# A two-layer transformer kernel on one Trainium2 core: layer 1's attention in pairs of units, and a new order of loads and steps in its end part

## The chip, the cores and the metric

The kernel runs on one core of a Trainium2 chip. A core has five engines with a queue each: TensorE (PE; its weight loads are listed as PEld), VectorE (DVE), ScalarE (ACT), GpSimd (POOL) and SyncE (SP). Each engine executes its own list of instructions in order, and waits on semaphores for the others. Matmuls write to PSUM, which has eight banks of 2 KB for each of 128 partitions. The metric is the time of one launch on the device in microseconds (us); lower is better.

## What is computed

The reference is two transformer layers on x of shape (8, 256, 128), all in float32. A small matmul gives six vectors per batch element and layer, a shift s, a scale c and a gate g for each half:

```python
h = _layernorm(x, axis=-1) * (1 + ca) + sa
x = x + ga * _L0_attn_ref(h, ...)            # 16 heads of width 8, causal
h = _layernorm(x, axis=-1) * (1 + cb) + sb
x = x + gb * _L0_ffn_ref(h, ...)             # shared expert and the best 2 of 8
...
x = x + ga * _L1_attn_ref(h, w_q, w_k, w_v, w_o)   # 16 heads of width 64, causal
...
x = x + gb * _L1_ffn_ref(h, ...)             # h, shared expert, and the best 2 of 16
```

Layer 1's attention, which the change is about, is

```python
q = einsum('bsd,hqd->bhsq', x, w_q); k = ...; v = ...
scores = einsum('bhsq,bhtq->bhst', q, k)
weights = softmax(where(causal, -inf, scores) / sqrt(64), axis=-1)
cat = einsum('bhst,bhtv->bhsv', weights, v).transpose(0, 2, 1, 3).reshape(b, s, -1)
return einsum('bsf,df->bsd', cat, w_o)
```

Layer 1's expert network has 16 experts of width 64, gates from a sigmoid, and the two best chosen per token.

## The kernel before, in words

x lies in SBUF in four tiles of 512 tokens (two batch elements each), and h, the normalised input, lies turned, with features on the partitions. The two layers run one after the other; from layer 0's attention on, the order on every engine is the order in which the program writes its steps (`tc.manual_schedule()`).

**Layer 1's attention.** A unit is a quarter of the heads (four) of one batch element; B = 8 elements of 4 units give N = 32 units, numbered n = 4b + u. For each unit there are these steps:

- `project_qk1(b, u)`: q and k for four heads, 128x128 weights against 256 columns of h; each result takes one PSUM bank of the two with tag "p". VectorE copies q to SBUF and ScalarE copies k.
- `project_v1(b, u)`: a quarter of v, one matmul of 512 columns into a "p" bank; ScalarE copies it.
- `scores1(b, u, between)`: for each m of two pairs of heads, two matmuls side by side in the array (64 rows each) for each of two blocks of keys, into a tile "sc" of two banks (tag "s", two buffers: four banks). ScalarE takes the Exp into "pt", and POOL sets what lies above the diagonal to zero (`causal`, line 804). `between` holds steps which are put between the four causal instructions in POOL's list: gathers and scatters, set up with `at_head`.
- `values1(b, u)`: o = v times pt, 64 columns of the array each (tag "o", one bank), and the sums of pt with a matrix of ones, 32 columns each (tag "sum", one bank, which adds up over the four units of b). VectorE copies o to "ou".
- `reciprocals1(b)` takes r = 1 / sum (VectorE), writes r to DRAM ("rd") and reads it back spread over the partitions ("rb", one buffer); `judge(r)` keeps a flag on its range. `normalise1(b, u)` multiplies ou by rb, and `finish1(b)` multiplies by the output weights (y, line 1639, 32 matmuls) and adds to x.

The loop over n writes: scores1(n), project_qk1(n+2), the `early` steps, values1(n-1), project_v1(n+2), reciprocals1 where a batch element is done, the `ends` steps. `early` and `ends` hold layer 0's last combines, the layernorms (`measure` and `normalise` on VectorE and ScalarE, `modulate` with transposes "nt" on TensorE and the way back to SBUF on VectorE), the normalisations and projections of finished elements, and the router: `route1` is a generator whose steps (`go`) are the logits "lg", the choice of two experts on VectorE, their ranks "rk", and scatters of the tokens into xs, sorted by expert (POOL, line 916).

**The end part.** Tokens of the first six elements go through 40 tiles of 128 sorted rows, four tiles to a step m = 0 to 9 (NQ = 10). The first 16 tiles belong to the 16 experts with weights in SBUF. The others belong to whichever expert has more rows; `tables_steps` works out their experts (widx) and rows (rowi). `fetch_rows1(m)` loads rows (SyncE), `find_rows1(m)` loads the rows' places into SyncE's registers one by one, and `fetch_weights1(m)` loads experts' weights of 128 KB: for m = 4, 5 by SyncE with a register loaded ahead of each DMA, for m = 6 to 9 by POOL with indirect DMAs (line 1030). Then `turn1(m)` (transposes, and the fetch of rows m+4), `hidden1(m)`, `project_tiles(m)` (writes ys by SyncE). When all of ys is written, POOL gathers each token's two rows (`gather1`, 24 indirect DMAs, line 1038) and `combine1` adds them. The last two elements go through all experts densely: `norms`, `go6`/`go7` (their routers), `gate_rows`, `dense_hidden`, `dense_gate`, `dense_project`, `ffn1_add`. After the loop all these steps stand in one list written out by hand.

Of the kernel before, what the change touches and what calls it, by code (L numbers as in the profile page):

```python
# [16 lines left out]
P = 128  # L17
# [540 lines left out]
def fast_path(ctx: ExitStack, tc: tile.TileContext, i: dict, out: bass.AP, bad: bass.AP):  # L558
# [292 lines left out]
    class Sorted:  # L851
# [163 lines left out]
        def row_start(self, d):  # L1015

            return nc.values_load(
                self.rowi[0:1, d : d + 1], engines=[mybir.EngineType.SP], min_val=0,
                max_val=self.ne * self.cap - P,
                skip_runtime_bounds_check_because="clamped above, and not negative",  # L1020
            )

        def load_rows(self, xg, d, r=None):

            r = self.row_start(d) if r is None else r
            nc.sync.dma_start(out=xg, in_=self.xs[bass.ds(r, P), :])
# [500 lines left out]
    def project_qk1(b, u):  # L1527

        hb = batch_cols(h, b)
        for what, copy in (("q", nc.vector.tensor_copy), ("k", nc.scalar.copy)):  # L1530
            ps_ = ps_ln([P, 2, S], f"{what}p1_{b}_{u}")
            for n in range(2):
                nc.tensor.matmul(  # L1533
                    out=ps_[:, n, :], lhsT=w1[f"w{what}1"][:, bass.ts(2 * u + n, P)], rhs=hb, start=True, stop=True
                )
            st1[what, b, u] = lp.tile([P, 2, S], F32, tag=what, bufs=3, name=f"{what}1_{b}_{u}")
            copy(st1[what, b, u], ps_)  # L1537
# [16 lines left out]
    def scores1(b, u, between):  # L1554

        q, k = st1.pop(("q", b, u)), st1.pop(("k", b, u))
        for m in range(2):
            c = 2 * u + m
            sc = pp.tile([P, 2, 512], F32, tag="s", name=f"sc1_{b}_{c}")
            pt = lp.tile([P, 2, 384], F32, tag="pt", bufs=4, name=f"pt1_{b}_{c}")  # L1560
# [14 lines left out]
    def values1(b, u):  # L1575
        v = st1["v", b, u // 2]
        if u == 0:
            st1["s", b] = pp.tile([P, S], F32, tag="sum", bufs=1, name=f"sum1_{b}")
            st1["ou", b] = lp.tile([P, 2, 4, S], F32, tag="ou", name=f"ou1_{b}")
        s = st1["s", b]  # L1580
        o = pp.tile([P, 2, S], F32, tag="o", bufs=1, name=f"o1_{b}_{u}")
        pts = [st1.pop(("pt", b, 2 * u + m)) for m in range(2)]
        for m in range(2):
            for kb, cols, qs in blocks:
                for n in range(2):
# [3 lines left out]
                    )  # L1589

        for kb, cols, qs in blocks:
# [6 lines left out]
        nc.vector.tensor_copy(st1["ou", b][:, :, u, :], o)  # L1598

    def reciprocals1(b):  # L1600
# [14 lines left out]
        judge(r)  # L1615
# [112 lines left out]
    def find_rows1(m):  # L1728

        starts.extend(z1.row_start(4 * m + t - E1) for t in range(4))  # L1730

    def fetch_weights1(m):
# [3 lines left out]
        for t in range(4):  # L1736
            d = 4 * m + t - E1
            if m > 5:
                z1.load_weights(wt[:, t, :], i["wpk1"], d)
                continue  # L1740
            r = nc.values_load(
                z1.widx[0:1, d : d + 1], engines=[mybir.EngineType.SP], min_val=0, max_val=(E1 - 1) * P,
                skip_runtime_bounds_check_because="an expert's number, 128 times",
            )
            nc.sync.dma_start(out=wt[:, t, :], in_=i["wpk1"][bass.ds(r, P), :])
# [135 lines left out]
    def gather1(j):  # L1881
        k, n = divmod(j, 3)
        if n == 0:
            sums["yg", k] = lp.tile([P, 3, 2, P], F32, tag="pt", bufs=4, name=f"yg1_{k}")
# [39 lines left out]
    project_v1(0, 0)  # L1924
    project_qk1(0, 1)
    project_v1(0, 1)
    measure, normalise, modulate = layernorm_parts(0, md[1], SA, CA, "1a1", ps_ln, tiles=range(2, TT))
    at_end(0, lambda: combine(1), measure)
    at(1, normalise)
    at_end(1, modulate)  # L1930
# [3 lines left out]
    at_end(1, lambda: combine(2))  # L1934
    at_end(2, lambda: combine(3))
    for w in range(1, NW):
        n = 8 * w
        if w > 1:
            for k in range(4):
                at_head(n - 13 + k, 3, lambda w=w, k=k: gather(2 * w + k // 2, k % 2))  # L1940
            at_end(n - 9, lambda w=w: combine(2 * w))
            at_end(n - 8, lambda w=w: combine(2 * w + 1))
        measure, normalise, modulate = first_norm(w)
        n -= 7 if w > 1 else 6
        at_end(n, measure)
        at(n + 1, normalise)
        at_end(n + 1, modulate)
    for b in range(B - 1):
        n = 4 * b + 6 if b < B - 2 else N - 1
        at(n, *[lambda b=b, u=u: normalise1(b, u) for u in range(4)])  # L1950
        at_end(n, lambda b=b: finish1(b))
    for bs in ((0, 2), (2, 2), (4, 1), (5, 1)):
        n = 4 * sum(bs) + 2
        measure, normalise, modulate, tokens, add = norm1(bs)
        go = one(route1(bs))
        at_end(n, measure)
        at(n + 1, normalise)
        at_end(n + 1, modulate, tokens)
        at(n + 2, go)
        at_end(n + 2, go, go, go, go)  # L1960
        at_end(n + 3, go)
# [222 lines left out]
```

## Time and profile before

| | |
|---|---|
| median of 14 runs | 639.73 us (637.33 to 644.71) |
| the profiled execution | 641.42 us |
| its span, first to last instruction | 639.4 us |
| mean granted TensorE clock | 0.948 |
| packets and bytes moved by DMA | 51377, 85.45 MB, mean 134 GB/s |

Stages of the span: layer 0 until about 280 us, layer 1's attention from the first scores at 289.98 to 538.9, the 40 tiles until the last ys lands at about 585.6, and the gathers and the dense part from there to the end. From 340 to 500 us TensorE is busy for 158.1 of 160 us (in the stretch 404 to 436 for 30.53 of 32), at the full clock.

In the page a line of instructions is: start in us, length in us, engine, line of the program, operation, output tile <- input tiles, rows*columns of the array, shape, count, and in square brackets the engine's idle time before it with what ended it. Neighbouring instructions of one kind are merged. SPq and POOLq are the queues' own DMA issues. A float32 matmul shows as two MATMUL instructions.

### The profile page before, as it was taken

How to read it: one execution, taken by the hardware profiler on the slowest of the kernel's cores; microseconds unless marked ns; L12 is line 12 of the kernel's file. 1: busy time of each engine (PE TensorE's matmuls, PEld its weight loads, DVE VectorE, ACT ScalarE, POOL GpSimd, SP SyncE). 2: the span in 40 equal slices, each digit the busy share in tenths (PEclk: the TensorE clock that was granted, in tenths of full speed). 3: DMA queues.
4: the chain of work that ended last, by engine and by line, in shares of the span. 5: the costliest groups of instructions: out<-in, count | busy, mean ns of one | idle time of the engine just before them, and what ended most of it. 6: DMA issues, size and time to landing. Idle time of an engine off the chain costs nothing.

```text
span 639.4 us, 12934 instructions
## 1 busy us (share of the span) xinstructions
PE 565.2 (88%) x4903; PEld 402.6 (63%) x4903; DVE 350.1 (55%) x1055; ACT 288.7 (45%) x502; POOL 307.0 (48%) x454
## 2 busy tenths in 40 slices
PE   3798988988869999969999999999999996797973
PEld 3444544455569999756667676767776765675443
DVE  4335658677663222145743666566647575546486
ACT  2477665555505555426633453344434441442230
POOL 7234457576631444136561144752355647612773
PEclk9999898888989999989999999999999999889797
DMA  8999970012033999522030203030303035742441
GB/s 285 350 408 395 389 262 22 14 55 92 26 116 92 330 328 332 169 99 83 26 88 6 68 10 84 30 80 1 68 23 80 18 72 168 206 118 78 105 100 71
DMA packets 51377, 85.45 MB, mean 134 GB/s; under 512 B 6428, under 2 KB 30108, under 8 KB 50156
## 3 DMA queue, kind: packets, MB, share of 16 engines
q1 hardware_dynamic: 42140, 57.67, 28.2%
q0 software_dynamic: 9168, 26.88, 13.3%
q8 instruction: 40, 0.66, 0.4%
q14 instruction: 29, 0.24, 0.1%
HBM read 53.46 MB, written 31.07 MB: 132 GB/s over the span
## 4 chain that ended last, share of the span: by engine, by line
PE 39%; DVE 7%; POOL 3%; issue 3%; DMA 2%; ACT 2%; SPq 1%; DVEq 0%; POOLq 0%; ACTq 0%
PE sc L1564 7%; PE o L1586 6%; PE qp L1533 5%; PE vp L1546 5%; PE kp L1533 4%; PE y L1639 4%; POOL yg L1038 3%; PE sum L1594 3%; DMA yg<-ys,yidx 1%; PE gu L1771 1%; DMA xg<-xs 1%; PE xT L1760 1%; DVE tc L1894 1%; DVE a L1838 1%; PE rp L1627 1%
## 5 line engine op out<-in xcount | busy, mean ns | idle before, releaser
L804 POOL TENSOR_SCALAR_AFFINE_SELECT pt<-pt 128x256 f32<-128x256 f32 (+1 forms) x176 | 89.0, 531 | 135.4 <-ACT pt L1567 80.0
L1038 POOL DMA_INDIRECT yg<-ys,yidx x56 | 53.4, 954 | 54.3 <-issue 34.1
L1030 POOL DMA_INDIRECT wt<-in_wpk_dram,widx x47 | 44.3, 942 | 54.8 <-PE xT L1312 48.5
L1567 ACT ACTIVATE pt<-sc 128x768 f32<-128x768 f32 x64 | 48.4, 808 | 25.5 <-PE sc L1564 25.4
L1134 ACT ACTIVATE pt<-sc 128x1024 f32<-128x1024 f32 x48 | 46.5, 1020 | 28.0 <-PE sc L1130 27.9
L1323 ACT ACTIVATE hst<-hp,wt 128x128 f32<-128x128 f32 x136 | 38.8, 368 | 29.8 <-ACT hst L1323 20.9
L1564 PEld LDWEIGHTS sc<-q,k 64*128 64x128 f32 x512 | 41.6, 187 | 16.4 <-issue 11.4
L1564 PE MATMUL sc<-q,k 64*128 64x256 f32 (+1 forms) x512 | 50.5, 337 | 0.0
L1586 PE MATMUL o<-pt,v 128*64 128x256 f32 (+1 forms) x512 | 48.7, 332 | 1.7 <-POOL pt L804 1.7
L1549 ACT COPY v<-vp 128x512 f32<-128x512 f32 x32 | 18.7, 585 | 67.5 <-PE vp L1546 56.7
L1586 PEld LDWEIGHTS o<-pt,v 128*64 128x64 f32 x512 | 31.9, 137 | 19.6 <-POOL pt L804 5.5
L1333 DVE COPY ysb<-yt 128x128 f32<-128x128 f32 x39 | 11.4, 292 | 59.0 <-PE yt L1329 59.0
L1537 DVE COPY q<-qp 128x512 f32<-128x512 f32 x32 | 22.0, 688 | 38.5 <-PE qp L1533 38.5
L1321 PE MATMUL hp<-xTs,wt 128*128 128x128 f32 x272 | 36.7, 278 | 2.3 <-DMA wt<-in_wpk_dram,widx 1.4
L1533 PE MATMUL qp<-h,wq 128*128 128x256 f32 x128 | 37.1, 414 | 1.3 <-DVE sh L1282 1.3
L916 POOL DMA_INDIRECT xs<-ht0b,idx x32 | 31.5, 983 | 13.0 <-issue 4.6
L1546 PE MATMUL vp<-wv,h 128*128 128x512 f32 x64 | 35.9, 643 | 1.1 <-DVE q L1537 1.1
L1130 PE MATMUL sc<-qm,k 32*128 32x512 f32 x192 | 34.4, 745 | 2.6 <-ACT pt L1134 1.8
L1329 PE MATMUL yt<-wt,hst 128*128 128x128 f32 x272 | 35.8, 276 | 0.0
L1321 PEld LDWEIGHTS hp<-xTs,wt 128*128 128x128 f32 x272 | 33.0, 192 | 3.9 <-DVE xTs L1314 1.5
L1533 PE MATMUL kp<-h,wk 128*128 128x256 f32 x128 | 33.5, 385 | 0.0
L1329 PEld LDWEIGHTS yt<-wt,hst 128*128 128x128 f32 x272 | 33.0, 192 | 0.0
(292 smaller groups left out, 1172.5 us busy)
## 6 DMA issues: line engine op xcount, KB each, us to landing
xs<-zero SPq DMA_DIRECT2D x1, 12288.0 KB
xs<-zero SPq DMA_DIRECT2D x1, 8192.0 KB
rb<-rd SPq DMA_DIRECT2D x14, 512.0 KB
mdb<-mrd SPq DMA_DIRECT2D x2, 2048.0 KB
xg<-xs SPq DMA_DIRECT2D x63, 64.0 KB
wst<-in_wpk_dram SPq DMA_DIRECT2D x5, 514.0 KB
ys<-ysb SPq DMA_DIRECT2D x10, 256.0 KB
ys<-ysb SPq DMA_DIRECT2D x39, 64.0 KB
```

What stands on the lines that cost most here:

```text
L804: nc.gpsimd.affine_select(out=pt, in_=pt, compare_op=ALU.is_ge, fill=0.0, base=0, pattern=[[0, pt.shape[1]], [1, P]], channel_multiplier=-1,)
L1030: nc.gpsimd.indirect_dma_start(out=wt, out_offset=None, in_=packed, in_offset=bass.IndirectOffsetOnAxis(ap=self.widx[:, d : d + 1], axis=0),)
L1038: nc.gpsimd.indirect_dma_start(out=yg[:, k, :], out_offset=None, in_=self.ys[:, :], in_offset=bass.IndirectOffsetOnAxis(ap=self.yidx[:, j, ...
L1134: nc.scalar.activation(pt[:, bass.ts(half, 2), :], sc, AF.Exp)
L1321: nc.tensor.matmul(out=hp[:, c, :], lhsT=wt[:, bass.ts(c, P)], rhs=xT, start=True, stop=True)
L1323: nc.scalar.activation(hs[:, c, :], hp[:, c, :], AF.Gelu_apprx_tanh, bias=wt[:, WB + c : WB + c + 1])
L1329: nc.tensor.matmul(out=y, lhsT=hs[:, c, :], rhs=wt[:, bass.ds(WF + c * P, P)], start=(c == 0), stop=(c == FC - 1))
L1533: nc.tensor.matmul(out=ps_[:, n, :], lhsT=w1[f"w{what}1"][:, bass.ts(2 * u + n, P)], rhs=hb, start=True, stop=True)
L1546: nc.tensor.matmul(out=vp, lhsT=hb[:, bass.ts(j, P)], rhs=w1["wv1"][:, bass.ts(half, 512)], start=True, stop=True)
L1564: nc.tensor.matmul(out=sc[:, n, cols], lhsT=k[r, m, bass.ts(kb, P)], rhs=q[r, m, qs], start=True, stop=True)
L1567: nc.scalar.activation(pt, sc[:, :, 0:384], AF.Exp, scale=1.0 / math.sqrt(D1))
L1586: nc.tensor.matmul(out=o[bass.ts(n, D1), m, qs], lhsT=v[:, kb, bass.ts(4 * (u % 2) + 2 * m + n, D1)], rhs=pts[m][:, n, cols], start=(kb == ...
```

## The change

The loop goes over N/2 stages; stage s has n = 2s + 1. In one stage the whole (128x128) matmuls of two units stand together, then the tiled ones. The extra steps get numbered slots in a stage (`place(stage, slot, ...)`, done by `do`) in place of `early` and `ends`. The sums of pt get a function of their own, `sums1`, and q and k of odd units share one "s" tile instead of two "p" banks. "pt" has six buffers instead of four.

```diff
-        for what, copy in (("q", nc.vector.tensor_copy), ("k", nc.scalar.copy)):
-            ps_ = ps_ln([P, 2, S], f"{what}p1_{b}_{u}")
+        if u % 2:
+            qk = pp.tile([P, 2, 2, S], F32, tag="s", name=f"qkp1_{b}_{u}")
+        ps_ = {}
+        for k, what in enumerate("qk"):
+            ps_[what] = qk[:, k] if u % 2 else ps_ln([P, 2, S], f"{what}p1_{b}_{u}")
...
-    for n in range(N):
-        b, u = divmod(n, 4)
-        scores1(b, u, behind.pop(n, {}))
...
+    scores1(0, 0, behind.pop(0, {}))
...
+    do(-1, 4)
+    for stage in range(N // 2):
+        n = 2 * stage + 1
+        more = n + 1 < N
         b, u = divmod(n, 4)
         scores1(b, u, behind.pop(n, {}))
+        do(stage, 0)
+        if more:
+            project_qk1(*divmod(n + 1, 4))
             project_qk1(*divmod(n + 2, 4))
+        do(stage, 1)
+        if more:
+            project_v1(*divmod(n + 1, 4))
             project_v1(*divmod(n + 2, 4))
+        do(stage, 2)
+        if more:
+            scores1(*divmod(n + 1, 4), behind.pop(n + 1, {}))
+        values1(b, u - 1)
+        do(stage, 3)
+        sums1(b, u - 1)
+        if more:
+            sums1(b, u)
+            if u == 3:
+                reciprocals1(b)
+            values1(b, u)
+            if u == 3:
+                judge(st1["r", b])
+        do(stage, 4)
```

The slots of the steps that the prediction speaks of (w counts tiles of x, b batch elements, bs the spans of the second layernorm and router):

```diff
+    place(-1, 4, lambda: combine(1), measure)
+    place(0, 0, normalise)
+    place(0, 2, modulate)
...
+        n = 4 * w - 5 if w > 1 else 1
...
+            place(n, 2, lambda w=w: combine(2 * w))
+            place(n, 4, lambda w=w: combine(2 * w + 1))
...
+        place(n, 4, measure)
+        place(n + 1, 3, normalise)
+        place(n + 2, 0, modulate)
...
+        n = 2 * b + 2
+        for u in range(4):
+            place(n, 2 + u // 2, lambda b=b, u=u: normalise1(b, u))
+        if b < B - 2:
+            place(*((n, 4) if b in (1, 3, 4, 5) else (n + 1, 2)), lambda b=b: finish1(b))
...
+        n = 2 * sum(bs)
+        soon = bs[0] == B - 3
...
+        place(n, 4, measure)
+        if soon:
+            place(n + 1, 1, normalise)
+            place(n + 1, 2, modulate, tokens)
+            place(n + 1, 4, go)
+            place(n + 2, 0, go, go, go, go)
+            n += 2
+        else:
+            place(n + 1, 3, normalise)
+            place(n + 2, 0, modulate, tokens)
+            for k in range(1, 6):
+                place(n + 2, k, go)
+            n += 3
+        place(n, 1 if bs[0] < 4 else 2, go)
```

SyncE's registers are loaded four with one call, all weights from m = 4 on are loaded by SyncE, and rows 0 to 3 come ahead of the first weights:

```diff
-        starts.extend(z1.row_start(4 * m + t - E1) for t in range(4))
+        starts.extend(z1.row_starts(4 * m - E1, 4))
...
-            if m > 5:
-                z1.load_weights(wt[:, t, :], i["wpk1"], d)
-                continue
-            r = nc.values_load(
-                z1.widx[0:1, d : d + 1], ...
+            if t == 0:
+                _, rs = nc.values_load_multi_w_load_instructions(
+                    z1.widx[0:1, d : d + 4], ...
...
-    at_end(29, tables, lambda: fetch_weights1(4), lambda: fetch_weights1(5))
-    at_end(30, *[lambda m=m: fetch_rows1(m) for m in range(4)], *[lambda m=m: find_rows1(m) for m in range(4, NQ)])
+    place(14, 3, tables)
+    place(14, 3, *[lambda f=f, m=m: f(m) for f, m in (
+        (fetch_rows1, 0), (fetch_rows1, 1), (fetch_rows1, 2), (fetch_rows1, 3), (fetch_weights1, 4), (fetch_weights1, 5),
+    )], *[lambda m=m: find_rows1(m) for m in range(4, NQ)],
+          lambda: fetch_weights1(6))
+    place(15, 0, lambda: finish1(B - 2))
```

In the list behind the loop the order changes: weights 7 stand behind the first `project_tiles`, 8 and 9 behind the second; `hidden1(0)` stands between the first two turns; the second part of `tables` behind `turn1(4)`; `hidden1(7)` ahead of `turn1(8)`. Behind the last `project_tiles` come the gathers, `shared_hidden(0)`, `go6`, `finish1(B - 1)` and the last layernorm; `shared_project(2)` stands behind `dense_hidden(1)` and the last router step; `dense_gate`, `dense_project` and `combine1` are written one by one, from two gates ahead of `dense_hidden(7)` on, in place of a loop of gate, project and two combines.

## The prediction on record

> **What bounds the kernel now.** First the page's busy shares and its chain that ended last: TensorE is busy for 88% of the span and carries the chain, and the longest lines of the chain are layer 1's attention.
>
> ```profile
> PE 565.2 (88%) x4903; PEld 402.6 (63%) x4903; DVE 350.1 (55%) x1055; ACT 288.7 (45%) x502; POOL 307.0 (48%) x454
> ...
> PE 39%; DVE 7%; POOL 3%; issue 3%; DMA 2%; ACT 2%; SPq 1%; DVEq 0%; POOLq 0%; ACTq 0%
> PE sc L1564 7%; PE o L1586 6%; PE qp L1533 5%; PE vp L1546 5%; PE kp L1533 4%; PE y L1639 4%; POOL yg L1038 3%; PE sum L1594 3%; DMA yg<-ys,yidx 1%; PE gu L1771 1%; DMA xg<-xs 1%; PE xT L1760 1%; DVE tc L1894 1%; DVE a L1838 1%; PE rp L1627 1%
> ```
>
> Then TensorE's timeline of one unit in the steady state (start, length, instructions):
>
> ```profile
> 340.00 1.58 PE L1564 MATMUL sc<-q,k 64*128 64x256 f32 x16
> 341.50 1.13 PE L1533 MATMUL qp<-h,wq 128*128 128x256 f32 x4
> 342.47 1.02 PE L1533 MATMUL kp<-h,wk 128*128 128x256 f32 x4
> 343.43 1.52 PE L1586 MATMUL o<-pt,v 128*64 128x256 f32 x16
> 344.88 0.86 PE L1594 MATMUL sum<-pt,on 128*32 128x256 f32 x16
> ```
>
> The next unit's scores start at 346.72, so a unit takes 6.72 us and no idle is named: the stage is as long as TensorE's own list. Where waits do stand in it, they look like this:
>
> ```profile
> 365.85 1.13 PE L1546 MATMUL vp<-wv,h 128*128 128x512 f32 x2
> 366.81 0.85 PE L764 MATMUL nt1a<-ident,xn1a 128*128 128x128 f32 x4
> 368.02 4.21 PE L1639 MATMUL y<-wo,ou 128*128 128x128 f32 x32 [0.36 <-DVE ou L1619]
> 372.16 1.58 PE L1564 MATMUL sc<-q,k 64*128 64x256 f32 x16
> ```
>
> After the attention the chain is another. SyncE issues the tiles' weights and rows one after the other (line 1745, 1721, 1026), the first transposes wait for rows, and TensorE's clock falls after the pauses (0.75 in the second stretch: columns are stretch, busy times of PE, PEld, DVE, ACT, POOL, clock, DMA share, GB/s):
>
> ```profile
> 530.55 7.05 SPq L1745 DMA_DIRECT2D wt<-in_wpk_dram  x8
> 537.70 2.05 SPq L1721 DMA_DIRECT2D xg<-xs  x4
> 547.49 6.21 SPq L1026 DMA_DIRECT2D xg<-xs  x12
> ```
>
> ```profile
> 541.23 0.66 PE L1760 MATMUL xT<-ident,xg 128*128 128x128 f32 x4 [2.33 <-DMA xg<-xs]
> 543.73 1.09 PE L1760 MATMUL xT<-ident,xg 128*128 128x128 f32 x4 [1.84 <-DMA xg<-xs]
> ```
>
> ```profile
> 541.20:563.00 21.80, 16.67 (x152) 13.29 (x154) 10.41 (x33) 9.34 (x16) 13.84 (x16) 0.75 0.75 214
> 586.60:617.70 31.10, 25.07 (x84) 11.18 (x80) 17.45 (x48) 11.38 (x19) 23.99 (x26) 0.84 0.46 108
> ```
>
> From 586.58 POOL's 24 gathers of 1.25 us (line 1038) set the pace, then VectorE.
>
> The sum is made against the profiled execution: 641.42 us, of which the span is 639.4. The median is 639.73, 0.26% less.
>
> **1. Fewer changes of the matmul's shape.** Inside one shape a 256-column matmul follows the last after 0.215 us (kp: four take 0.86, and 0.96 to the next shape). So a unit streams for 1.29 (sc, eight pairs) + 1.72 (qp, kp) + 1.29 (o) + 0.65 (sum) + 0.86 (vp) = 5.82, and 0.91 of its 6.73 is lost at five changes. The rows split it: vp takes 0.96 to the next start when a whole matmul follows (365.85 to 366.81) and 1.055 when scores follow, so leaving a shape costs 0.095; entering costs 0.105 with 128 columns of weights (qp 0.97 against kp's 0.86 + 0.095), by the same subtraction 0.05 with 64 (o) and 0.025 with 32 (sum). Before, a pair of units pays ten changes, 1.82. After, whole, sc, sc, o, sum, o: six exits 0.57, entries 0.105 + 0.21 + 0.10 + 0.025 = 0.44, and the pairs' stagger 0.09: 1.10. That saves 0.73 in each of 15 full stages: **-11.0**. Four output projections y and one router stand in slot 4, between values and scores, and break a run of tiled matmuls: 5 x 0.20 = **+1.0**.
>
> The Trainium skill, "TensorE: Matmul & The Clock Gate", section "The mechanism", speaks against half of this: weights load beside running matmuls only where the row group differs. By it the entries would be paid between whole matmuls too, only the four exits would be saved, 0.38 a stage and 5.7 in all. The rows disagree: whole matmuls in a row, all in one row group, follow each other after 0.215 with a weight load of 0.19 each. I take 11.0.
>
> **2. Waits that go.** In the timeline from 302 to Z (the start of unit 30's scores, 523.53 before) TensorE loses beyond shape changes 1.16 twice at nt and y as shown (366.8, 432.8), 1.2 before vp at 425.06, 0.4 at each of nt 378.8, nt 444.9 and rk 522.9, 0.15 at nt 315.5: **-4.9**. The layernorm's normalise now stands a whole stage ahead of its transposes, and values stand ten microseconds behind their POOL masks, so I let all of these go.
>
> **3. Waits that come**, from the order of each queue. A stage without waits: sc(n) 0 to 1.5, qk to 5.05, v to 6.8, sc(n+1) to 8.4, o(n-1) to 9.8, both sums to 11.26, o(n) to 12.7.
> - Transposes in slot 0 take one of two "p" banks. VectorE's evacuation ends 1.74 after their start (0.75 to its start, 0.99 for two); kp wants that bank 1.3 after: 0.45, four times. At stage 3 the projection needs the same h: 0.8. Together 2.6.
> - Stages 4 and 8: VectorE does r 1.76, ou 0.69, judge 0.88, combine 2.5 and measure 1.15 from 11.4 on, so q's copy ends at 6.4 of the next stage and is seen at 6.5, and v wants its bank at 5.05: 2 x 1.45 = 2.9. Behind them only q(n+2) is queued, which has time.
> - rb lands 8.6 after its reciprocal ends (517.1 to 525.8 in the completion records), so at 9.05 of the next stage; two normalise1 follow to 10.3, then ou, and o(n) wants its bank at 11.26: no wait. Where normalise delays r by 1.2 (stages 5, 9, 11) the transposes of the next stage cover two; 0.8 in all.
> - The router's steps ahead of q in stage 14: 0.35; y behind normalise1: 0.4.
> - No cost: odd units' q and k take a bank pair of the scores, free after the first Exp (about 2.0, wanted at 3.2); six "pt" buffers hold three units, which are what is alive.
>
> Sum **+7.0**; none at the lower end. The first two scores now follow each other without work between, so the second waits for the first's Exp with its table load (1.28), and VectorE's normalise stands before q: **+1.8**.
>
> **4. Up to Z.** One unit's values and sums (1.45 + 0.79) now come after Z: **-2.2**. Z moves by -11.0 + 1.0 - 4.9 + 7.0 + 1.8 - 2.2 = **-8.3**.
>
> **5. From Z to the first gather** (63.05 before, at 586.58). Unit 31's first masks cost no wait now (1.8 at 530.59 before), but two normalise1 stand before the router's indices, so the first scatter goes at Z+3.6 instead of 1.7 and the last lands at 13.2 (11.35 before: 534.88). Rows 0 to 3 now come first on SP and hold all weights behind them. Prices on SP: a DMA with its registers loaded 0.52 (12 in 6.21); a register load 0.32 (24 between 539.75 and 547.49). What a load of four costs isn't shown: 0.32 if the time is the instruction's, 1.28 if it is the register's. I take 0.32, nearest to a load's round trip. Then rows 0-3 end at 15.4, weights 4 and 5 at 20.2, six finds at 22.1, weights 6 at 24.5, rows 4 at 26.6, landing 1.9 later at 28.5: where turn1(4) runs today (552.05), though SP started seven later. TensorE is ready there at 24.6 and idles. On: rows 7 land at 37.5, rows 8 behind weights 8 and 9 at 44.7, rows 9 at 47.1 (turn1(9) today 46.9). Then hidden, projections, spread (3.9) and the last ys store reach the first gather at 59.9. The pause before rows 8 is 3.5, and pauses of that size brought half clock (0.66 in 540 to 550): 3.4 us of matmuls twice as long, 63.3. So **+0.25**: POOL loses 16 loads, which nobody waited for, and SP gains them.
>
> Of a load of four registers, the Trainium skill, "Runtime: NRT & Kernel Launch", section "Instruction fetch mechanics", says about 200 ns per register even in bulk. By it a load would take an estimated 0.8 and twelve would add 5.8 to this sum. Its figure is for loads from HBM; no run here shows one.
>
> **6. From the first gather to the end** (54.8 before). The 24 gathers stay 30 us. shared_project(2) moves behind the router (1.16 sooner), but finish1 comes behind shared_hidden(0); the gates' rows land 0.5 sooner. VectorE's list behind them (16.7 us, 617.68 to 634.4) loses about 1.0 of gaps: **-1.5**.
>
> **Sum:** -8.3 + 0.25 - 1.5 = -9.55: 631.9 for this execution, 630.2 for the median.
>
> **Rivals.**
> - *The queues keep up*: the 7.0 of point 3 don't come: 623.2. For it: VectorE is busy for only 62% of 340 to 500. Against: each wait above follows from the order in one queue, and busy shares are means.
> - *SP becomes the bound, slower than before*: a load of four costs 1.28; twelve stand before rows 9: 12 x 0.96 = 11.5, and the longer pauses bring one more half-clock spell, 3.4: 645.1. It decides from about 1.1 us per load (9.55 / 12 + 0.32). For it: the third row of SP above is one queue, already full for 20 us. Against: TensorE's earlier start leaves it slack.
> - *The loss isn't by shape*, so grouping saves nothing: +10.0, 640.2. Against: nothing is lost between qp and kp, nor at vp to nt.
> - *The clock stays up* in the tail: -3.4: 626.8.
>
> **Chances:** forecast 0.50, queues keep up 0.20, clock 0.13, SP 0.10, no saving by shape 0.05, something else 0.02. The range 622 to 639 leaves out SP, most of "no saving" and the low end of the first rival. About 0.3% (1.9 us) is what a measurement can tell. Faster by more 0.84, within 0.07, slower 0.09.
>
> **What would show it.** Right: a stage of 12.7 in TensorE's timeline with qp, kp, qp, kp, vp, vp in one run; small waits at kp behind nt and at vp in stages 4 and 8; about 0.32 for a load of four; a pause before the fifth and ninth turn; gathers still 1.25 apart. Wrong: stages of 13.4 without named waits (point 1); waits on ScalarE or POOL in the stages; SP pausing on scatters well past Z+13 or loads over 1 us (point 5).

## The result, and the profile after

The changed kernel takes **649.11 us** (median of 10 runs), the kernel before 639.41 (median of 47) in the same comparison: ratio 1.0168, 95% interval 1.0138 to 1.0198. The forecast was 630.2, faster. Both profiled executions, cut at the first scores of the attention, at unit 30's scores (Z), at the first gather (G) and at the issue of the last output DMA:

| us | to the first scores | to Z | Z to G | G to the last output DMA | behind it |
|---|---|---|---|---|---|
| before (span 639.4) | 290.0 | 233.55 | 63.05 | 47.84 | 4.93 |
| after (span 648.8) | 289.7 | 236.57 | 64.36 | 47.28 | 10.90 |
| difference | -0.3 | +3.0 | +1.3 | -0.6 | +6.0 |
| predicted | in the next column | -8.3 | +0.25 | -1.5 | in the column before |

So the loss has two places, the attention and the very end. The page of the changed kernel, busy shares and chain, against the first lines of before:

```profile
PE 557.3 (86%) x4903; PEld 405.0 (62%) x4903; DVE 344.4 (53%) x1055; ACT 286.6 (44%) x502; POOL 295.1 (45%) x438
...
PE 19%; DMA 11%; DVE 9%; POOL 7%; issue 4%; SPq 3%; ACT 3%; DVEq 0%; POOLq 0%; ACTq 0%
DMA rb<-rd 7%; POOL yg L1039 5%; PE y L1648 4%; PE sc L1570 3%; PE o L1590 3%; PE qkp L1538 2%; DMA rd<-r 2%; DVE r L1612 2%; DVE ou L1628 2%; PE vp L1552 1%; SPq L1752 1%; PE kp L1538 1%; PE qp L1538 1%; PE sum L1605 1%; PE gu L1778 1%
```

TensorE's share of the chain fell from 39% to 19%, and its largest line is now the transfer of `rb`, which wasn't in the chain of before. The longest waits in the attention (engine, line, releaser: us in total, times, longest), TensorE's first and then VectorE's on `rb`:

```profile
PE o L1590 <- DVE ou L1594: 5.6, 6, 1.9
PE kp L1538 <- DVE h L767: 2.0, 4, 0.7
PE rk L902 <- ACT v L1555: 1.8, 1, 1.8
PE sc L1570 <- ACT pt L1573: 1.3, 1, 1.3
PE qp L1538 <- DVE h L767: 0.6, 1, 0.6
```

```profile
DVE ou L1628 <- DMA rb<-rd: 18.8, 6, 3.8
```

How the two hang together shows in one stage, TensorE's timeline and then VectorE's:

```profile
488.60 1.52 PE L1590 MATMUL o<-pt,v 128*64 128x256 f32 x16
490.05 1.51 PE L1605 MATMUL sum<-pt,on 128*32 128x256 f32 x32
493.48 2.27 PE L1590 MATMUL o<-pt,v 128*64 128x256 f32 x16 [1.92 <-DVE ou L1594]
```

```profile
489.12 1.65 DVE L1628 TENSOR_TENSOR ou<-ou,rb 128x512 f32<-128x512 f32 x2 [3.29 <-DMA rb<-rd]
490.69 0.17 DVE L1703 TENSOR_SCALAR p<-p 128x32 f32<-128x32 f32 x1
...
492.61 0.21 DVE L839 SCALAR_TENSOR_TENSOR tw<-s,p 128x32 f32<-128x32 f32 x1
492.75 0.68 DVE L1594 COPY ou<-o 128x512 f32<-128x512 f32 x1
```

The first `o` ends at 490.1. Its copy, which frees the only bank of `o`, runs at 492.75: ahead of it in VectorE's queue stand two `normalise1` that wait for `rb` until 489.12, and behind those the router's steps, 2.06 us long. The second `o` starts the moment the copy has read its bank. It also takes 2.27 us in place of 1.52, as TensorE runs at half clock for a while behind this wait. The same happens once more, at 511 (columns as in the prediction: the granted clock is the third number from the end):

```profile
493.40:500.30 6.90, 6.82 (x48) 5.87 (x48) 2.77 (x9) 0.00 (x0) 0.17 (x1) 0.75 0.04 12
511.00:515.00 4.00, 4.00 (x36) 2.47 (x36) 0.41 (x1) 2.78 (x3) 3.73 (x6) 0.57 0.07 20
```

The end of the span, VectorE's last step and SyncE's last DMA, first in the kernel before and then in the changed one:

```profile
627.63 0.20 DVE L1908 TENSOR_SCALAR bad<-good_cnt,most 1x1 int32<-1x1 f32 x1 [0.84 <-PE good_cnt L1907]
634.42 0.33 SPq L2087 DMA_DIRECT2D out_dram<-x  x1
```

```profile
637.81 0.20 DVE L1915 TENSOR_SCALAR bad<-good_cnt,most 1x1 int32<-1x1 f32 x1
637.92 0.33 SPq L2152 DMA_DIRECT2D out_dram<-x  x1
```

After these two, nothing that counts as work follows in the changed kernel, for 10.6 us. `bad` is the flag that `judge` collects. At the kernel's end every engine loads it and branches on it, to a general path if it is set. Before, the flag's last step (a matmul of one column, `good_cnt`, and this comparison) stood inside the loop of projections; GpSimd loaded the flag at 628.17, and the span ended 11.2 later. After, the step is the last line of the list, behind the last addition; GpSimd loads it at 638.04, and the span ends 10.8 later.

### The profile page after: what moved, and what is told of

It reads as the page before. It is cut to its first block, busy times and chain, and to the rows that moved or that the text cites. A ratio compares the mean times of both kernels' runs of the same rounds, so it can differ in the third digit from the quotient of the medians.

```text
span 648.8 us, 12920 instructions
## 1 busy us (share of the span) xinstructions
PE 557.3 (86%) x4903; PEld 405.0 (62%) x4903; DVE 344.4 (53%) x1055; ACT 286.6 (44%) x502; POOL 295.1 (45%) x438
## 4 chain that ended last, share of the span: by engine, by line
PE 19%; DMA 11%; DVE 9%; POOL 7%; issue 4%; SPq 3%; ACT 3%; DVEq 0%; POOLq 0%; ACTq 0%
DMA rb<-rd 7%; POOL yg L1039 5%; PE y L1648 4%; PE sc L1570 3%; PE o L1590 3%; PE qkp L1538 2%; DMA rd<-r 2%; DVE r L1612 2%; DVE ou L1628 2%; PE vp L1552 1%; SPq L1752 1%; PE kp L1538 1%; PE qp L1538 1%; PE sum L1605 1%; PE gu L1778 1%
## 5 line engine op out<-in xcount | busy, mean ns | idle before, releaser
L804 POOL TENSOR_SCALAR_AFFINE_SELECT pt<-pt 128x256 f32<-128x256 f32 (+1 forms) x176 | 91.4, 543 | 159.6 <-ACT pt L1573 103.2
L1039 POOL DMA_INDIRECT yg<-ys,yidx x56 | 54.8, 978 | 57.2 <-DMA ys<-ysb 34.8
L1590 PE MATMUL o<-pt,v 128*64 128x256 f32 (+1 forms) x512 | 50.7, 342 | 5.6 <-DVE ou L1594 5.6
L1031 POOL DMA_INDIRECT wt<-in_wpk_dram,widx x31 | 29.0, 935 | 51.8 <-PE xT L1313 50.3
L1594 DVE COPY ou<-o 128x512 f32<-128x512 f32 x32 | 21.6, 674 | 29.9 <-PE o L1590 29.9
L916 POOL DMA_INDIRECT xs<-ht,idx x24 | 23.8, 993 | 19.0 <-DVE idx L911 10.5
L1648 PEld LDWEIGHTS y<-wo,ou 128*128 128x128 f32 x256 | 30.1, 197 | 3.6 <-ACT v L1555 1.8
L1552 PE MATMUL vp<-wv,h 128*128 128x512 f32 x64 | 31.5, 607 | 0.6 <-DVE q L1543 0.6
L1648 PE MATMUL y<-wo,ou 128*128 128x128 f32 x256 | 31.6, 283 | 0.2 <-ACT v L1555 0.2
```

The costliest lines, as they stand in the source:

```text
L804: nc.gpsimd.affine_select(out=pt, in_=pt, compare_op=ALU.is_ge, fill=0.0, base=0, pattern=[[0, pt.shape[1]], [1, P]], channel_multiplier=-1,)
L916: self.apart(nc.gpsimd.indirect_dma_start(out=self.xs[:, :], out_offset=bass.IndirectOffsetOnAxis(ap=idx[:, j, k : k + 1], axis=0), in_=to ...
L1039: nc.gpsimd.indirect_dma_start(out=yg[:, k, :], out_offset=None, in_=self.ys[:, :], in_offset=bass.IndirectOffsetOnAxis(ap=self.yidx[:, j, ...
L1552: nc.tensor.matmul(out=vp, lhsT=hb[:, bass.ts(j, P)], rhs=w1["wv1"][:, bass.ts(half, 512)], start=True, stop=True)
L1590: nc.tensor.matmul(out=o[bass.ts(n, D1), m, qs], lhsT=v[:, kb, bass.ts(4 * (u % 2) + 2 * m + n, D1)], rhs=pts[m][:, n, cols], start=(kb == ...
L1648: nc.tensor.matmul(out=y[:, j, :], lhsT=aT[:, c % 2, c // 2, bass.ts(j, P)], rhs=w1["wo1"][:, c, :], start=(c == 0), stop=(c == NC1 - 1),)
```

## The experiments

Theory after the trace: VectorE's queue behind `rb` costs the attention its gain, and the flag's late branch costs the end; in the tail, loads of four registers gain and something takes the gain back. Rivals stand with each run.

**Two kinds of chip.** The runs fell on several chips. Where the kernel before takes 639 to 642 us (the runs of the second and third group below, and the comparison above) I call them calm. On four others it takes 670 to 672 (medians; the runs lie between 667 and 676), and the time is lost in the tail. There TensorE stops inside one tile's eight equal matmuls, with no releaser (kernel of the run e14_tail_fours_again):

```profile
554.14 0.54 PE L1784 MATMUL gu<-xTs,wg 128*64 128x128 f32 x5 [1.39 <-issue]
554.86 0.33 PE L1784 MATMUL gu<-xTs,wg 128*64 128x128 f32 x2 [0.18 <-issue]
556.99 0.37 PE L1784 MATMUL gu<-xTs,wg 128*64 128x128 f32 x1 [1.80 <-issue]
```

The stretch from G to the last output DMA takes 61 to 66 us there and 46 to 48 on the calm chips. VectorE stops there too without a releaser, while the gathers run (e16_weights_first_sp: 7.49 us before 602.21 and 6.59 before 611.31), and GpSimd's gathers keep their 1.25. That GpSimd's transfers themselves take longer there doesn't show in the gathers: their last packet ends 1.2 us behind the last gather's issue in e16_weights_first_sp, and 2.9 in the changed kernel on a calm chip. Ratios are compared only within one kind, and times only within one group of runs.

### First group (before: 670.16)

**e1_flag.** The flag's last step goes back between the projections:

```diff
     dense_gate(7)
     dense_project(5)
+    next(judged, None)
...
     ffn1_add(LAST)
-    next(judged, None)
```

> The changed kernel with one step moved: the last step of the flag (one matmul and a comparison) stands again ahead of the last four sums, as before, instead of behind the last addition. Theory (the branch behind the flag sets the end): in the changed kernel GpSimd loads the flag at 638.04 and the span ends 10.75 later; in the kernel before it loaded it at 628.17 and the span ended 11.2 later. With the flag early GpSimd loads it as soon as its own last addition is done (633.2 to 634.4), so the run ends 4 to 5 us sooner, at about 644.5 against 649.1, and the last output DMA stays where it is. Rival (the last output DMA and VectorE's list set the end): no change, 649. Second rival (the matmul of the flag on TensorE and its wait hold back the last projections): 649 to 650.

**e2_slot3.** All four `normalise1` go behind the copy of ou(n-1):

```diff
-            place(n, 2 + u // 2, lambda b=b, u=u: normalise1(b, u))
+            place(n, 3, lambda b=b, u=u: normalise1(b, u))
```

> The changed kernel with all four normalise1 of a batch in slot 3 of their stage, so that in VectorE's queue they stand behind the copy of ou of the unit before and not ahead of it. Theory (VectorE waits for rb and, behind it, the copy of ou that frees the one bank of o): the waits of TensorE between the sums and o, 9.1 us in nine stages of the changed kernel, fall under 1.5, and unit 30's scores start at 518 to 520 instead of 526.3; total 641 to 643 against 649.1. Rival (VectorE has too much work in these stages, whatever the order): the waits move to q's copy or to y, and the total stays within 2 us of 649. Rival (the transfer of rb itself is late): waits appear at y and at the next stage, 646 to 649.

**e3_both.** Both edits.

> Both edits together: the four normalise1 in slot 3 and the flag's last step ahead of the last four sums. If the two causes are separate they add: 649.1 - 4.6 - 7 = 637.5, between 636 and 639, a little under the 639.4 of the kernel before. If either is only cover for the other (the end waits for something else once the attention is shorter), 641 to 644.

**e4_old_tail.** Grouped attention of the changed kernel, everything behind it, registers and weights as before.

> The grouped attention of the changed kernel with the tail of the kernel before: registers one at a time, weights from the sixth group on by GpSimd, rows behind weights 4 and 5, the old order of the steps behind the attention. Theory (the grouping costs 2.8 us by its waits, the tail's new order 1 to 1.5 up to the first gather and 6 behind it): unit 30's scores start at about 526, the total is about 642, 7 under the changed kernel. Rival (SyncE's queue was the gain of the new tail, and the old tail cannot follow the later or earlier scatters): 646 or more. Rival (the loss is all in the tail): 639 or less.

Measured: e1_flag 662.58 (ratio 0.9867, 0.980 to 0.9935), e2_slot3 661.38 (0.9834, 0.977 to 0.990), e3_both **656.14** (0.979, 0.975 to 0.983), e4_old_tail 679.77 (1.015, 1.010 to 1.020). The absolute expectations missed for the chip. By medians the flag is worth 661.38 - 656.14 = 5.2 and slot 3 662.58 - 656.14 = 6.4, about what the theory had. With four runs each the intervals overlap, so the sizes rest on the traces and on the later groups; whether the two add can't be told, as the changed kernel wasn't run on this chip. In e3_both the longest waits of TensorE in the attention are:

```profile
PE kp L1538 <- DVE h L767: 2.9, 4, 1.6
PE rk L902 <- ACT v L1555: 1.8, 1, 1.8
PE sc L1570 <- ACT pt L1573: 1.3, 1, 1.3
PE qp L1538 <- DVE h L767: 1.0, 1, 1.0
```

"o <- DVE ou" is gone, with the same work on VectorE, so it was the order and not the load. From the first scores to Z it takes 230.94 against 238.72 in e1_flag (an estimated 1.7 of this is a spell of 3.4 us at half clock, which only e1_flag has). The same stage in e3_both:

```profile
488.92 0.69 DVE L1594 COPY ou<-o 128x512 f32<-128x512 f32 x1 [0.35 <-PE o L1590]
489.53 3.02 DVE L1628 TENSOR_TENSOR ou<-ou,rb 128x512 f32<-128x512 f32 x4
```

The copy now runs right behind its matmuls, and `rb` has landed by the time the four multiplications come up. The stretch behind the last output DMA is 10.52 with the late flag (e2_slot3) and 5.30 to 5.59 with the early one (e3_both, e1_flag). e4_old_tail decides nothing: its Z to G took 75.87, by the pauses above.

### Second group (before: 641.88, calm)

**c_after.** The changed kernel itself, no edit.

> The changed kernel as it is, on the chip of this call, as the measure for the others. On the chip of the first comparison it took 1.0168 times the kernel before. On the chip of the last four runs the kernel before took 670 instead of 639, and from the differences of those runs (5.2 for the flag) the changed kernel would have taken about 668 there. Theory (the change trades GpSimd's weights for SyncE's, and what that is worth depends on how long a chip's software transfers take): 1.012 to 1.02 where the kernel before takes about 639, about 0.996 where it takes about 670. Rival (the same ratio everywhere): 1.017.

**e5_singles.** One register per load:

```diff
-        starts.extend(z1.row_starts(4 * m - E1, 4))
+        starts.extend(z1.row_starts(4 * m + t - E1, 1)[0] for t in range(4))
```

and the same in `fetch_weights1`.

> The changed kernel with the registers loaded one at a time again (24 for the rows, 24 for the weights of the groups 4 to 9), all else as it is. A load of four took 0.30 to 0.35 in the changed kernel's trace, four single ones 1.28 in the trace before. Theory (SyncE's queue stands before rows 4 and rows 8): nine loads of four stand before rows 4 and twelve before rows 9, so rows 4 come 8.5 us later and the first gather 8 to 13 us later; total 8 to 13 above the changed kernel. Rival (the gathers wait for something else, the queue has slack): under 3 above it.

**e6_rk_bank.** e3_both, and the router's ranks of two spans in the bank of `o`:

```diff
-            yield from z1.place_steps(2 * bs[0], nt, tokens1[bs], ps_ln)
+            yield from z1.place_steps(2 * bs[0], nt, tokens1[bs], ps_ln if bs[0] not in (4, 5) else ps_o)
```

> The flag's last step early, all normalise1 in slot 3, and in addition the ranks of the last two sparse routers (rk) go to the bank of o instead of one of the two banks that the values' projections use. In the run with the first two edits TensorE waited 1.80 and 0.63 us for ScalarE's copy of v before rk. Theory (rk waits for the bank of the second last projection): both waits go, and unit 30's scores start 2.0 to 2.8 us sooner than in that run (230.9 after the first scores there, 228.1 to 228.9 here); against the changed kernel on the same chip the total falls by 12 to 14 us (5.2 flag, 6.4 slot 3, 2 here). Rival (rk then waits for VectorE's work in front of it, or o for rk's reader): the waits stay under another name and the gain on the changed kernel is 10 to 12.

**e7_pool_weights.** The changed kernel with GpSimd's weights:

```diff
+            if m > 5:
+                z1.load_weights(wt[:, t, :], i["wpk1"], d)
+                continue
```

> The changed kernel with the weights of groups 6 to 9 loaded by GpSimd again (16 indirect loads of 1.25 us in its queue), in the new order and place. Theory (these loads were not waited for before, and SyncE's share is in the way of rows 4 and 8): within 2 us of the changed kernel where the kernel before takes about 639. [...] Rival (GpSimd's 20 us push the scatters or norms behind them): 5 or more above it on every chip.

Measured: c_after 650.78 (1.0158, 1.0111 to 1.0205): the result again. e5_singles 657.39 (1.028, 1.021 to 1.035): 6.6 slower by medians, where 8 to 13 was expected, its Z to G 76.0 against 63.85. So SyncE's queue is on the path, and the loads of four carry the new tail. e6_rk_bank **636.95** (0.9931, 0.990 to 0.996): 13.8 under the changed kernel, a total within what was expected, and faster than before. The place of rk isn't where that comes from, though: its wait of 1.80 became two others, as the rival had it:

```profile
500.84 0.18 PE L903 MATMUL rk<-seen,allb 128*128 128x32 bf16 x1 [0.46 <-POOL seen L899]
502.45 0.49 PE L764 MATMUL nt1b<-ident,xn1b 128*128 128x128 f32 x2 [1.43 <-DVE xn1b L755]
```

e7_pool_weights 648.76 (1.011, 1.0065 to 1.0154), its Z to G 60.25: the 16 loads that I moved in my head at no cost cost 3.6 in that stretch when SyncE issues them; in the total the gain is 2.0, inside the intervals.

### Third group (before: 639.03, calm)

**e8_mended.** e6_rk_bank with GpSimd's weights, as in e7.

> The three mended places together with GpSimd's loads of the weights 6 to 9: flag early, all normalise1 in slot 3, rk in the bank of o, weights of groups 6 to 9 by GpSimd. On the chip of the last four runs the first three gave 0.9931 of the kernel before (636.95), and GpSimd's weights brought the first gather to 60.25 behind unit 30's scores against 63.85 in the changed kernel. Theory (SyncE's weights cost 3 to 3.6 on the way to the first gather): 0.987 to 0.990 where the kernel before takes about 640, about 633; on a chip where it takes 670 slower than that. Rival (GpSimd's loads and the earlier Z collide, and the flag, which GpSimd reads, comes later): 0.993 or more.

**e9_before_late_flag.** The kernel *before* with the flag's step behind `ffn1_add(LAST)`.

> The kernel before with one edit of the change alone: the flag's last step behind the last addition and not between the projections. Theory (from GpSimd's load of the flag to the end of the span there are 10.1 to 11.9 us in each of the profiles so far, whatever the rest does): GpSimd loads the flag at about 634.5 instead of 628.2 and the time rises by 5 to 6.3 us, ratio 1.008 to 1.010. Rival (the last output DMA sets the end, and the late end of the changed kernel came from its list of sums): under 1.002.

**e10_mended_old_tail.** e2_slot3 with rk in the bank of `o`, and the tail of e4_old_tail.

> The grouped attention with all normalise1 in slot 3 and rk in the bank of o, and behind it the tail of the kernel before as a whole (single registers, GpSimd's weights, old order and the flag in its old place). Theory (the mended grouping gains 5.3 up to unit 30's scores: 228.3 against 233.55; the old tail takes 63 from there to the first gather and 52.8 behind it): 0.991 to 0.994 where the kernel before takes about 640. Rival (the old tail needs the old attention's scatters and its first rows come late, as in the run with the old tail): 1.0 or more.

**e11_before_fours.** The kernel *before* with `row_starts(4 * m - E1, 4)` and one load per four weights for groups 4 and 5.

> The kernel before with one part of the change alone: registers loaded four at a time by SyncE (six loads for the rows instead of 24, two for weights 4 and 5 instead of 8), nothing else. SyncE's queue then is 5.7 us shorter between rows 3 and rows 4 and 1.9 shorter before rows 0. Theory (the queue stands before rows 4 and on TensorE's path): the first gather 2 to 5 us sooner, ratio 0.992 to 0.997. Rival (TensorE is the bound from the first turn on, the rows are early enough): 0.999 to 1.001.

Measured: e8_mended **631.84** (0.989, 0.984 to 0.994), as expected, Z to G 59.56: against e6_rk_bank's 63.45 a second pair, after e7, in which SyncE's weights cost 3.6 to 3.9 there. e9_before_late_flag 644.0 (1.0081, 1.0043 to 1.0119): one line moved costs 5.0 us, in a kernel where nothing else is changed. e11_before_fours 633.25 (0.9911, 0.988 to 0.994), its Z to G 56.2: the loads of four alone take the kernel before down by 5.8, a little more than I expected. Much of that comes by the clock: TensorE waits 0.83 and 0.26 us for the first two turns' rows in place of 2.33 and 1.84, and its granted clock from Z to G is 0.97 in place of 0.89, an estimated 5 us of the stretch. e10_mended_old_tail fell to its rival: 640.32 (1.0018), Z to G 67.96.

### Two more kernels and a variant, on chips with pauses

**e12_mended_tail_fours**: e10 with loads of four. **e13_weights_first**: e8 with weights 4 and 5 ahead of rows 0 to 3. **e14_tail_fours_again** and **e17_tail_fours_third** are e12's kernel, **e15_weights_first_again** is e13's. **e16_weights_first_sp** is e13 with SyncE's weights.

```diff
-    place(14, 3, tables)
-    place(14, 3, *[lambda f=f, m=m: f(m) for f, m in (
-        (fetch_rows1, 0), (fetch_rows1, 1), (fetch_rows1, 2), (fetch_rows1, 3), (fetch_weights1, 4), (fetch_weights1, 5),
-    )], ...
+    place(14, 3, tables, lambda: fetch_weights1(4), lambda: fetch_weights1(5))
+    place(14, 4, *[lambda m=m: fetch_rows1(m) for m in range(4)], ...
```

> The grouped attention with all normalise1 in slot 3 and rk in the bank of o, and behind it the old tail with one part of the change: registers four at a time. Weights 6 to 9 by GpSimd, weights 4 and 5 ahead of rows 0 to 3, the old order of TensorE's steps. Theory (the two gains are separate: 3.5 to 5.3 up to unit 30's scores, 6.9 behind it, where the kernel before with fours alone came to 56.2 up to the first gather): first gather 56 to 59 behind unit 30's scores, ratio 0.982 to 0.986, 627.5 to 630 where the kernel before takes 639. Rival (with the shorter attention SyncE and the scatters become the bound again, as the old tail with single loads showed with 67.96): 0.989 or more.

> The mended kernel with GpSimd's weights 6 to 9 (0.989 of the kernel before, first gather at 59.56 behind unit 30's scores), with one more part undone: on SyncE the weights 4 and 5 stand ahead of rows 0 to 3 again, so that they are issued while the scatters still land. Theory (rows 0 to 3 first hold 4.6 us of weights behind the last scatter and so rows 4, which come at 21.5 behind unit 30's scores instead of 17.3 in the kernel before with fours): first gather at 56 to 57.5, ratio 0.983 to 0.986. Rival (the order of TensorE's steps behind the attention makes the difference, not SyncE's order): 59 to 60, ratio 0.988 to 0.990.

> The same kernel as in the last but one run (mended attention, old tail, registers four at a time, weights by GpSimd, weights 4 and 5 ahead of rows 0 to 3). That run fell on a chip on which the kernel before takes 671 and TensorE's tail pauses for up to ten microseconds without a named cause, which covers what was to be measured. Where the kernel before takes about 640, theory (two separate gains): first gather 56 to 59 behind unit 30's scores, ratio 0.982 to 0.986. Rival (SyncE and the scatters become the bound with the shorter attention): 60 or more, ratio 0.989 or more.

> The same kernel as in the last run (mended attention, new order of TensorE's tail, weights 4 and 5 ahead of rows 0 to 3 on SyncE), for the same reason. Theory (rows ahead of weights costs 3 to 4): first gather at 56 to 57.5, ratio 0.983 to 0.986. Rival (the order of TensorE's steps makes the difference): 59 to 60, ratio 0.988 to 0.990.

> The three mended places (flag early, all normalise1 in slot 3, rk in the bank of o), all further weights by SyncE as in the change, and weights 4 and 5 ahead of rows 0 to 3 on SyncE. The same without the last edit took 0.9931 of the kernel before where that takes 642, with the first gather at 63.45 behind unit 30's scores. Theory (rows ahead of weights costs 3 to 4 on SyncE's queue): first gather at 59.5 to 61, ratio 0.987 to 0.989 there. Rival (TensorE's order or its clock is the bound): 63 or more, 0.992 or more. On a chip where the kernel before takes 670 TensorE pauses while GpSimd's transfers run; this kernel has 16 fewer of those than the last four runs and should show 0.975 to 0.985 there.

> Mended attention with the whole old tail and registers four at a time, whose two runs so far fell on chips with unnamed pauses of TensorE (0.992 and 0.994 there). Where the kernel before takes about 640: theory (gains of attention and of loads of four add) first gather 56 to 59 behind unit 30's scores, ratio 0.982 to 0.986; rival (SyncE and the scatters become the bound) 60 or more, 0.989 or more. On a chip with the pauses: 0.992 to 0.994 again.

Before takes 670.8 to 671.6 in these three groups. e12's kernel: 0.9919, 0.9938, 0.9901; e13's: 0.9936, 0.9952; e16_weights_first_sp 0.9823 (0.979 to 0.986), Z to G 65.0. So these don't tell the calm prices apart. They do show SyncE's weights ahead on such chips: 0.9823 against 0.9936 (0.990 to 0.997) and 0.9952 (0.993 to 0.998) for the same kernel with GpSimd's weights, though on different chips. And e16's rows speak against what I expected of the order. VectorE's last step of `tables`, which gives the weights' indices, and SyncE behind it, in e11_before_fours (Z at 521.68), then in e16_weights_first_sp (Z at 518.66):

```profile
527.56 0.65 DVE L987 TENSOR_SCALAR widx<-expert_t,wnum_t 128x24 int32<-128x24 f32 x1
528.77 4.67 SPq L1747 DMA_DIRECT2D wt<-in_wpk_dram  x8
```

```profile
531.89 0.59 DVE L987 TENSOR_SCALAR widx<-expert_t,wnum_t 128x24 int32<-128x24 f32 x1
533.04 5.77 SPq L1755 DMA_DIRECT2D wt<-in_wpk_dram  x8
538.91 2.05 SPq L1733 DMA_DIRECT2D xg<-xs  x4
```

The weights can't start before the tables: Z+7.1 in the first, Z+14.4 in the second. With weights first the rows merely come later (Z+20.3, against Z+10.8 in e8_mended). So it is the tables that are late, and not the order on SyncE alone, because slot 3 of stage 14 puts them behind the four `normalise1` of the last `rb`: VectorE ends these at 531.5 in the changed kernel and starts the tables in the same moment, Z+5.2, where the kernel before starts them at Z+0.7. In the kernel before, and in e11, the weights are issued while the scatters still land. In the changed kernel:

```profile
536.54 0.24 DVE L987 TENSOR_SCALAR widx<-expert_t,wnum_t 128x24 int32<-128x24 f32 x1
539.04 2.06 SPq L1730 DMA_DIRECT2D xg<-xs  x4
541.99 4.84 SPq L1752 DMA_DIRECT2D wt<-in_wpk_dram  x8
```

tables end at Z+10.5, rows start at Z+12.8, weights behind them, and rows 4 are issued at Z+25.4 against Z+17.3 in e11. The 8.0 are weights 4 and 5 with their two loads (541.14 to 546.87: 5.7) and weights 6 with its load (2.7), which both stand between rows 3 and rows 4 now, less 0.4 for the rest.

e10_mended_old_tail is the nearest to a test of this: it has the tail of the kernel before, and the tables in slot 3. There they start at Z+6.7, the first weights are issued at Z+14.0 in place of Z+7.0, and G comes 4.9 later than before. But its scatters and normalisations differ too, and tables ahead of slot 3 weren't tried: that they are the cause isn't shown.

## Why the prediction was wrong

**Point 1, the shapes: right.** A stage without waits in the changed kernel goes from 308.96 to 321.68: 12.72 where 12.7 was worked out, with qp 0.97, kp 0.86, the pair 1.73, both vp 1.81, both sums 1.44. By the rule of the Trainium skill that I had weighed against it ("TensorE: Matmul & The Clock Gate", "The mechanism": weights load beside running matmuls only where the row group differs; the same section also allows for a background weight buffer) the stage would be an estimated 13.1. The rows disagree with that rule.

**Point 2, waits that go: right** as a list; each of them is gone or replaced by one of point 3. Its reason, that values stand ten microseconds behind their POOL masks, didn't hold in stage 0, where the sums wait for masks.

**Point 3, waits that come: the failing step.** I took 7.0, and 1.8 at the start. TensorE's starts beyond the clean stage's durations add up to about 20.5:

| place | predicted | measured |
|---|---|---|
| o(n) behind ou(n-1) and `rb` | 0.8 | 6.0 |
| y behind normalise1 | 0.4 | 0 |
| sums behind POOL's masks, stage 0 | 0 | 1.3 |
| half clock at 494 and 511 | 0 | 3.1 |
| transposes' bank | 2.6 | 3.1 |
| stages 4 and 8 | 2.9 | 0.7 |
| stages 12 to 14: rk, q | 0.35 | 4.0 |
| start, one vp | 1.8 | 2.3 |

The sentence that failed is "two normalise1 follow to 10.3, then ou, and o(n) wants its bank at 11.26: no wait". `rb` landed 8.8 to 9.0 behind its reciprocal in six of seven stages, where 8.6 was worked out, and once 10.2 (stage 8, a wait of 1.2). What I left out of the queue is what stands between: in the three stages where the router chooses (6, 10 and 12) its steps in slot 2, 2.1 to 2.4 us long, sit behind the same wait, and this is 4.2 of the 6.0. I had counted the router for stage 14 alone. With slot 3 this row is gone from the trace, and the time falls by about 6.4.

Two more rows had no term. In stages 12 to 14 the missing one was rk's bank: ScalarE loads a table for the layernorm's root (1.28) ahead of the copies of v that free it. And I priced no half clock inside the attention, which has none in the kernel before. This row is partly chance: c_after, the same kernel with the same long waits, has no half clock there, and 234.19 to Z in place of 236.57.

**Point 5: right in its sum, partly by luck.** +1.3 against +0.25; rows 4 landed at about Z+28.5, as worked out; a load of four takes 0.29 to 0.33, as taken, and not the estimated 0.8 by the figure per register of the Trainium skill ("Runtime: NRT & Kernel Launch", "Instruction fetch mechanics"), which is for loads from HBM. But large terms stood against each other in it: loads of four are worth 5.8 alone (e11), SyncE's weights take back 3.6 to 3.9 of the stretch (e7, e8), and the late tables, as argued above, the rest. My sum held them without giving any its own price; that "nobody waited for" GpSimd's loads was true, but SyncE's share of them was waited for. The 3.4 for a further spell of half clock isn't shown: the granted clock from Z to G is 0.89 before, and 0.87 and 0.92 in the two profiles of the changed kernel.

**Point 6: the other failing step.** To the last output DMA -0.6 instead of -1.5. Behind it +6.0, which isn't in the prediction: I went through VectorE's list for the length of its items and never asked who waits for the flag's comparison, which moved ten microseconds towards the end. e9 shows its price by itself, 5.0.

The misses add up: 11.05 to Z (both columns), 1.05 to G, 6.9 behind: 19.0, and -9.55 became +9.4 in the span. With both failing steps mended, e6_rk_bank is 4.9 under the kernel before and e8_mended 7.2, still short of 9.55; the other rows of the table are left in them. The rivals had the wrong causes too: SyncE's queue was there (e5), but as a gain kept, and the range left both places out.

## What to carry to other kernels

When a step that waits for a transfer is moved, list everything behind it in its engine's queue up to the next copy that frees a bank, in every stage with its own extra steps, and put copies that free a bank ahead of steps that wait. A value that decides a branch at the end has a price of its own: compute it ten microseconds early, so that GpSimd's steps behind the branch run beside the last work. Of two changes put against each other in one sum, try each alone: loads of four registers in the old kernel (0.991) and the mended grouping (0.993 with SyncE's weights, 0.989 with GpSimd's) were each faster than both kernels.

## What the runs showed of the hardware that was not expected

- From GpSimd's load of the flag to the end of the span there are 10.1 to 12.0 us in all 20 profiles, but for two reasons. In the six with a late flag GpSimd's own list ends last: in the changed kernel its branch to the next step takes 4.2, an INC_SWDGE_SEM 1.1 and its drain 3.7, to 647.97, while SyncE has drained at 644.99. In the 14 with an early flag the two lists end within 1.3 us of each other, in ten of them SyncE's, which starts with the last output, is the later (638.53 against 638.20 in the kernel before). There a still earlier flag should gain nothing; that wasn't run.
- TensorE's clock fell to half for one or two spells of 3.4 us inside the attention in 9 of the 17 profiles with grouped attention, and in none of the three with the old one; a spell costs an estimated 1.7 us.
- On four chips TensorE paused inside equal matmuls without a releaser in the tail, VectorE beside it, and the kernel before took 670 to 672 us instead of 639 to 642. What it is isn't settled. On them the changed kernel was not run; by e1_flag and the 5.2 of the flag it would take an estimated 0.994 to 0.997 of the kernel before there, so the sign of this change may depend on the chip, but with the interval of e1_flag (0.980 to 0.9935) that isn't clear of noise.
- The same code's stretches differ between profiles: to the first scores 285.6 to 296.0 over all, to Z 234.2 and 236.6 in two of the changed kernel (granted clock 1.00 and 0.99), Z to G 63.05 and 60.78 in before and e9 (0.89 and 0.94). Differences under 2.5 us in one stretch were not read from single profiles.
